# A routed expert kernel: the last 20 pairs of pages written twice, behind a branch on the page counts

## The chip, the cores and the metric

The kernel runs on one core of one Trainium2 chip. A core has TensorE (PE, matrix products), VectorE (DVE), ScalarE (ACT), GpSimd (POOL), SyncE (SP, here a queue of transfers) and 16 DMA engines. The metric is device time in microseconds (us), the median of the runs. One execution is taken by the hardware profiler; times inside it count from its first instruction.

## The reference

x has 8 batches of 512 tokens of width 256. A first layer (several normalizations with gathered tables and a small network) makes from each token a vector, and the second, of which the change speaks, sends it through 4 of 16 experts:

```python
probs = softmax(xf @ gate_w.T)
top_w, top_idx = top_k(probs, 4);  top_w /= sum(top_w)
h1, h3 = einsum('td,ehd->teh', xf, w1), einsum('td,ehd->teh', xf, w3)
eout = einsum('teh,edh->ted', silu(h1) * h3, w2)
x = x + sum over the 4 chosen of top_w * eout + a shared expert
```

All of it is in float32.

## The kernel before

The work has two stages. The first runs over the 8 batches, each of NJ = 4 tiles of 128 tokens; an order is planned by the class Plan, with costs and ranks, and written out for PE, DVE, ACT and SP. It ends with each tile's tokens routed. An expert's tokens stand in pages of 128 rows in a buffer xs_d in DRAM: a tile that fills an expert's page opens the next free one, so the pages of the experts lie mixed, in the order in which they were opened. The place of a token's k-th choice is in slot_all, and POOL scatters the normalized vectors there by indirect DMA. past_all keeps the number of pages opened so far. The experts can round up at most 16 x 127 rows, so after n tokens at most pages_after(n) = (4n + 16 x 127) // 128 pages are open: NPAGE = 143 at the end, and pages_for(b, j), which is 4t + 19 after tile t = 4b + j. Which expert owns a page is known only at run time, in page_e.

The second stage runs over pairs of pages, n_pair = 72 (the last has one page), in an order written out by hand in one loop. In pass i of the loop:

- experts(): before every other pair, PE, ACT and DVE load the experts' numbers of the next four pages into registers.
- load(): SP fetches four pages of xs_d (a quad), three quads ahead.
- turn(i + 2): PE transposes the pages (xt), ACT moves them out of PSUM with scale and bias (xtt).
- bring_weights(i + 2): ACT and DVE each copy one page's expert weights to a fixed place (wb).
- first(i): PE multiplies (hp), ACT makes silu, DVE multiplies the halves to g.
- second(i - 1): PE multiplies by w2 (yo), ACT copies yo to SBUF, and SP stores the two pages to ys_d.
- pick_weights(), in the first 32 passes: DVE gathers a tile's four routing weights.
- fetch(): POOL gathers 128 rows of ys_d for one tile and choice k by indirect DMA into a buffer yg. As its source is declared to be the first (pages_for - k) pages of ys_d, it waits for the stores of these and no others.
- weigh(): DVE adds weight times yg to x_all; after k = 0, SP writes the tile to the output.

There are 128 fetches in the order of tiles, k from 3 to 0. fetch_one() places the next one in the program if the pages that it needs are already stored at that place (stored[0]). It is called twice in each pass, before first() and before second(), and each fetch also waits for a mark there (xtt of pair i + 2, or g of pair i). There are eight buffers yg. weigh_due(i - 3) places the weigh() of the fetches that were placed three passes or more before. Each engine and each queue takes its instructions in order: on DVE a weigh() that waits for its fetch holds up the next wb and g, and on SP an output write that waits for weigh() holds up the next load and store. All indirect DMAs share POOL's queue, in order.

Line numbers of the rows below: L1515 xt, L1520 xtt, L1501 wb, L1539 hp, L1547 silu, L1559 yo, L1562 ACT's copy of yo, L1563 the store, L1447 the fetch, L1468 the output write; L192 is the helper through which all of DVE goes.

Of the kernel before, what the change touches and what calls it, by code (L numbers as in the profile page):

```python
# [9 lines left out]
F32 = mybir.dt.float32  # L10
BF16 = mybir.dt.bfloat16
I32 = mybir.dt.int32
AF = mybir.ActivationFunctionType
ALU = mybir.AluOpType
AX = mybir.AxisListType
# [4 lines left out]
P = 128  # L20
B, S, D = 8, 512, 256
E, HID, TOPK = 16, 128, 4
# [5 lines left out]
NJ = S // P  # L28
NC = D // P
# [23 lines left out]
def pages_for(b, j):  # L53

    return pages_after(b * S + (j + 1) * P)
# [11 lines left out]

NPAGE = pages_after(B * S)
QUAD = 4
NQUAD = -(-NPAGE // QUAD)  # L70


class Plan:
# [109 lines left out]
def adaln_ffn_kernel(ctx: ExitStack, tc: tile.TileContext, a: dict, out: bass.AP):  # L183
    nc = tc.nc
# [13 lines left out]
    vector = Recorded()  # L198
# [16 lines left out]
    pool_seq = {"single": None, "scatters": []}  # L215
# [24 lines left out]
    def start_after(name, i):  # L240

        tc.add_manual_dep(i.ins, marks[name], sync, reason="order of the transfers")
# [139 lines left out]
    if True:  # L382
# [49 lines left out]
        second = sp.tile([NROW, 4, D], BF16)  # L432
# [344 lines left out]
    with (  # L777
# [256 lines left out]

        flat = lambda v: v.rearrange("p a b -> p (a b)")
        by_tile = lambda v: v.rearrange("p e j -> p j e")
        turns = [0]

        def rank_d(b, g):

# [288 lines left out]
        for b in range(B):  # L1329
# [31 lines left out]
            t = b * T  # L1361
# [61 lines left out]
    def pick_weights(b, j):  # L1423
        eq = g2.tile([P, TOPK, E], F32, tag="eq", name=f"eq_{b}_{j}")
        vector.tensor_tensor(
            eq,
            pos_all[:, b, j].unsqueeze(1).to_broadcast([P, TOPK, E]),
            top_all[:, b, j, 0:TOPK].unsqueeze(2).to_broadcast([P, TOPK, E]),
            ALU.is_equal,
        )  # L1430
        vector.tensor_mul(
            eq, eq, ld[:, b * NJ + j].unsqueeze(1).to_broadcast([P, TOPK, E])
        )
        vector.reduce_sum(wk_all[:, b, j, :], eq, axis=AX.X)

    xs_v = xs_d.rearrange("(n p) d -> p n d", p=P)
    ys_v = ys_d.rearrange("(n p) d -> p n d", p=P)

    def pages_of_slot(b, j, k):

        return pages_for(b, j) - k

    def fetch(b, j, k, after):
        rows_ = pages_of_slot(b, j, k) * P
        yg = g2.tile([P, D], F32, tag="yg", name=f"yg_{b}_{j}_{k}", bufs=8)
        i = in_turn(
            nc.gpsimd.indirect_dma_start(  # L1447
                out=yg,
                out_offset=None,
                in_=ys_d[0:rows_, :],  # L1450
                in_offset=bass.IndirectOffsetOnAxis(ap=slot_all[:, b, j, k : k + 1], axis=0),
            )
        )
        if after:
            start_after(after, i)
        return yg

    def weigh(b, j, k, yg):
        vector.scalar_tensor_tensor(
            x_all[:, b, j, :],  # L1460
            yg,
            wk_all[:, b, j, k : k + 1],
            x_all[:, b, j, :],
            ALU.mult,
            ALU.add,
        )
        if k == 0:
            nc.sync.dma_start(out=out_v[b, :, j], in_=x_all[:, b, j])  # L1468
# [6 lines left out]

    def load(q):
        n = min(QUAD, NPAGE - q * QUAD)
        t = g2.tile([P, QUAD, D], F32, tag="xs", name=f"xs_{q}", bufs=4)
        nc.sync.dma_start(out=t[:, 0:n], in_=xs_v[:, q * QUAD : q * QUAD + n])
        loaded[q] = t  # L1480

    def experts(q):
        for engine in (PE, ACT, DVE):
            _, vs = nc.values_load_multi_w_load_instructions(
                page_e[0:1, q * QUAD : (q + 1) * QUAD],
                engines=[engine],
                min_val=0,
                max_val=(E - 1) * D,
                skip_runtime_bounds_check_because="an expert's number, or 0, times the width",
            )  # L1490
            values[q, engine] = vs
# [3 lines left out]
    def bring_weights(i):  # L1495
        for k, p in enumerate(pages_of(i)):
            v = values[p // QUAD, bring[k]][p % QUAD]
            brought[p] = g2.tile([P, NC, 2 * HID], F32, tag=f"wb{k}", name=f"wb_{p}", bufs=3)
            src = weights["w13"][:, :, bass.ds(v, 2 * HID)]
            if bring[k] == ACT:  # L1500
                nc.scalar.copy(brought[p], src)  # L1501
            else:
                vector.tensor_copy(brought[p], src)
# [4 lines left out]
    def turn(i):  # L1508

        src = loaded[2 * i // QUAD]  # L1510
        n = len(pages_of(i))
        pt = ps_t.tile([P, NC, 2, P], F32, tag=f"t{i % 2}", name=f"xt_{i}")
        for k, p in enumerate(pages_of(i)):
            for c in range(NC):
                nc.tensor.transpose(  # L1515
                    pt[:, c, k, :], src[:, p % QUAD, c * P : (c + 1) * P], ident
                )
        xt = g2.tile([P, NC, 2, P], F32, tag="xt", name=f"xtt_{i}", bufs=4)
        for c in range(NC):
            a_ = nc.scalar.activation(  # L1520
                xt[:, c, 0:n],
                pt[:, c, 0:n],
                AF.Identity,
                scale=vecs[:, V_INT_G, c : c + 1],
                bias=vecs[:, V_INT_BE, c : c + 1],
            )
        mark(("xt", i), a_)
        return xt
# [3 lines left out]
    def first(i, xt):  # L1532
        n = len(pages_of(i))
        pool, tag_ = ps_first[i % 4]
        ph = pool.tile([P, 2, 2, P], F32, tag=tag_, name=f"hp_{i}")
        for k, p in enumerate(pages_of(i)):
            for h in range(2):
                for c in range(NC):
                    nc.tensor.matmul(  # L1539
                        ph[:, h, k, :],  # L1540
                        brought[p][:, c, h * HID : (h + 1) * HID],
                        xt[:, c, k, :],
                        start=(c == 0),
                        stop=(c == NC - 1),
                    )
        g = g2.tile([P, 2, P], F32, tag="g", name=f"g_{i}", bufs=3)
        nc.scalar.activation(g[:, 0:n], ph[:, 0, 0:n, :], AF.Silu)  # L1547
        mark(("g", i), vector.tensor_mul(g[:, 0:n], g[:, 0:n], ph[:, 1, 0:n, :]))
        return g

    stored = [0]

    def second(i, g):
        n = len(pages_of(i))
        yo = g2.tile([P, 2, D], F32, tag="yo", name=f"yo_{i}", bufs=5)
        po = ps_o.tile([P, 2, D], F32, tag=f"o{i % 2}", name=f"yo_{i}")
        for k, p in enumerate(pages_of(i)):
            v = values[p // QUAD, PE][p % QUAD]
            nc.tensor.matmul(  # L1559
                po[:, k, :], g[:, k, :], w2[:, bass.ds(v, D)], start=True, stop=True  # L1560
            )
        nc.scalar.copy(yo[:, 0:n], po[:, 0:n])  # L1562
        nc.sync.dma_start(out=ys_v[:, 2 * i : 2 * i + n], in_=yo[:, 0:n])  # L1563
        stored[0] = 2 * i + n

    n_pair = -(-NPAGE // 2)
    for q in range(3):
        load(q)
    xt, g = {}, {}
    picks = [(b, j) for b in range(B) for j in range(NJ)]  # L1570
    fetches = [(b, j, k) for b in range(B) for j in range(NJ) for k in reversed(range(TOPK))]
    landed = []

    def fetch_one(i, after):

        if fetches:
            b, j, k = fetches[0]
            if stored[0] >= pages_of_slot(b, j, k) and (b, j) not in picks:
                landed.append((i, b, j, k, fetch(*fetches.pop(0), after)))
                return True  # L1580

    def weigh_due(by):

        while landed and landed[0][0] <= by:
            weigh(*landed.pop(0)[1:])

    experts(0)
    for t in range(2):
        bring_weights(t)
    for i in range(n_pair + 2):  # L1590
        if i % 2 == 0 and i // 2 + 1 < NQUAD:
            experts(i // 2 + 1)
        if i % 2 == 0 and i // 2 + 3 < NQUAD:
            load(i // 2 + 3)
        for t in range(3) if i == 0 else (i + 2,):
            if t < n_pair:
                xt[t] = turn(t)
        if i + 2 < n_pair:
            bring_weights(i + 2)

        if i + 2 < n_pair:
            fetch_one(i, ("xt", i + 2))
        if i < n_pair:
            g[i] = first(i, xt[i])
            fetch_one(i, ("g", i))
        if 0 <= i - 1 < n_pair:
            second(i - 1, g[i - 1])
        if picks:
            pick_weights(*picks.pop(0))
        weigh_due(i - 3 if i < n_pair else i)  # L1610
        while i >= n_pair and fetch_one(i, None):
            pass
    while landed or fetches:
        for _ in range(4):
            fetch_one(i, None)
        for _ in range(4):
            if len(landed) > 4 or landed and not fetches:
                weigh(*landed.pop(0)[1:])
# [58 lines left out]
```

## Time and profile before

| what | value |
|---|---|
| median of 3 runs | 506.04 us (505.32 to 507.46) |
| the profiled execution | 506.59 us |
| its span, first to last instruction | 504.9 us |
| mean granted clock of TensorE | 0.978 of full |
| PE busy | 476.4 us, 94% |
| DVE, ACT, POOL busy | 359.8, 291.4, 295.8 us |
| first and last fetch | 300.21 and 496.84 us |
| last weigh() begins | 499.73 us |

The span is a little shorter than the execution's own time, which holds what lies around it. The profile is read by stage: busy shares over the whole span mix a first stage with the pair loop (from about 267.5 us) and a tail behind PE's last product. A row of a timeline has the start, the length, the engine (PEld is the loading of weights, SPq a DMA issue on SP), line, operation, and in brackets how long the engine was idle before and what ended that.

### The profile page before, as it was taken

The page shows a single profiled execution, that of the slowest core. Times are in us where ns is not written, and L with a number is a line of the kernel's source. Part 1 is how long each engine was busy: PE and PEld are TensorE (multiplying, and loading weights), DVE is VectorE, ACT ScalarE, POOL GpSimd, SP SyncE. Part 2 cuts the span into 40 slices and gives each one's busy share as a digit, 9 for nine tenths or more (in the row PEclk, how much of TensorE's full clock was granted, in tenths as well). Part 3 has the DMA queues.
Part 4 walks back from the last instruction along what each step waited for, and adds up shares of the span by engine and source line. Part 5 has one row for each costly group of instructions (what it writes and reads, how often), then busy time and mean ns, then how long its engine had stood idle before and what let it go on. Part 6 is the DMA issues. An engine that isn't in the chain of part 4 may idle for free.

```text
span 504.9 us, 9488 instructions
## 1 busy us (share of the span) xinstructions
PE 476.4 (94%) x2764; PEld 358.8 (71%) x2764; DVE 359.8 (71%) x1459; ACT 291.4 (58%) x584; POOL 295.8 (59%) x320
## 2 busy tenths in 40 slices
PE   5989899999999999999998999999999999999970
PEld 2547556465656655456658999999999999999970
DVE  7997899999979788867846445777755455555552
ACT  5741643636654615133137777777777777777750
POOL 8615504777677777777750006556666576665673
PEclk8999899999999999999999999999999999999995
DMA  7749959879974758372235557889899899899773
GB/s 222 276 142 323 362 178 296 269 242 273 322 248 143 209 180 235 134 270 105 95 107 167 173 175 247 253 284 288 249 292 282 265 287 289 263 284 282 228 219 108
DMA packets 108153, 116.99 MB, mean 232 GB/s; under 512 B 9029, under 2 KB 95807, under 8 KB 108103
## 3 DMA queue, kind: packets, MB, share of 16 engines
q1 hardware_dynamic: 92942, 74.39, 47.5%
q0 software_dynamic: 14848, 41.96, 26.4%
q8 instruction: 22, 0.36, 0.3%
q14 instruction: 28, 0.23, 0.2%
q10 hardware_dynamic: 313, 0.05, 0.1%
HBM read 57.91 MB, written 58.46 MB: 230 GB/s over the span
## 4 chain that ended last, share of the span: by engine, by line
PE 67%; DVE 21%; DMA 7%; issue 2%; ACT 1%; POOL 1%; POOLq 0%; SPq 0%; DVEq 0%; ACTq 0%
PE hp L1539 25%; PE yo L1559 12%; PE ph L920 10%; PE xt L1515 6%; PE sh L753 5%; DVE pw L192 3%; DVE cat L192 3%; PE pz L940 3%; PE so L769 3%; DMA pw<-in_pw_dram,idx 2%; DMA x_all<-in_x_dram 1%; DVE st_x L192 1%; DVE st_h L192 1%; DMA xs_d<-z,slot_all 1%; DVE z L192 1%
## 5 line engine op out<-in xcount | busy, mean ns | idle before, releaser
L1447 POOL DMA_INDIRECT yg<-ys_d,slot_all x128 | 125.9, 983 | 111.0 <-ACT yo L1562 49.9
L1125 POOL DMA_INDIRECT xs_d<-z,slot_all x128 | 125.6, 982 | 41.9 <-issue 13.9
L1539 PE MATMUL hp<-xtt,wb 128*128 128x128 f32 x1144 | 139.5, 275 | 0.0
L1539 PEld LDWEIGHTS hp<-xtt,wb 128*128 128x128 f32 x1144 | 133.6, 192 | 0.1
L192 DVE TENSOR_TENSOR g<-g,hp 128x256 f32<-128x256 f32 x72 | 30.2, 419 | 82.9 <-ACT g L1547 82.8
L920 PE MATMUL ph<-cat,iws 128*128 128x512 f32 x192 | 88.9, 593 | 0.0
L1520 ACT ACTIVATE xtt<-xt,vecs 128x256 f32<-128x256 f32 x144 | 73.5, 566 | 3.2 <-PE xt L1515 3.2
L1559 PE MATMUL yo<-w,g 128*128 x286 | 73.7, 380 | 0.0
L192 DVE SCALAR_TENSOR_TENSOR x_all<-yg,wk_all,x_all 128x256 f32<-128x256 f32 x128 | 59.5, 482 | 10.7 <-DMA yg<-ys_d,slot_all 9.5
L920 PEld LDWEIGHTS ph<-cat,iws 128*128 128x128 f32 x192 | 35.9, 190 | 38.0 <-issue 33.2
L1562 ACT COPY yo<-yo 128x512 f32<-128x512 f32 x72 | 41.9, 583 | 33.9 <-PE yo L1559 26.2
L793 POOL DMA_INDIRECT pw<-in_pw_dram,idx x32 | 31.7, 992 | 44.6 <-ACT cat L903 32.1
L1559 PEld LDWEIGHTS yo<-w,g 128*128 128x128 f32 x286 | 48.8, 191 | 3.9 <-DVE g L192 0.2
L1501 ACT COPY wb<-w 128x512 f32 x72 | 44.6, 621 | 0.0
L1515 PE MATMUL xt<-ident,xs 128*128 128x128 f32 x286 | 42.9, 273 | 0.7 <-ACT xtt L1520 0.7
L1515 PEld LDWEIGHTS xt<-ident,xs 128*128 128x128 f32 x286 | 35.6, 141 | 7.9 <-ACT xtt L1520 0.9
L1547 ACT ACTIVATE g<-hp 128x256 f32<-128x256 f32 x72 | 27.6, 383 | 15.3 <-PE hp L1539 15.1
L940 PE MATMUL pz<-iw,hid 128*128 128x272 f32 x128 | 34.2, 404 | 0.0
L192 DVE COPY wb<-w 128x512 f32 x71 | 31.3, 443 | 3.4 <-issue 2.2
L820 ACT ACTIVATE z<-z,nb_z,rs_z 128x256 f32<-128x256 f32 x32 | 16.7, 588 | 27.7 <-DVE nb_z L192 27.7
L920 PE MATMUL ph<-catx,iws 128*128 128x512 f32 x64 | 30.3, 595 | 0.0
L820 ACT ACTIVATE pw<-pw,nb_h,rs_h 128x256 f32<-128x256 f32 x32 | 16.9, 590 | 21.4 <-DVE nb_h L192 21.3
(217 smaller groups left out, 668.9 us busy)
## 6 DMA issues: line engine op xcount, KB each, us to landing
ys_d<-yo SPq DMA_DIRECT2D x71, 256.0 KB, 2.2
xs<-xs_d SPq DMA_DIRECT2D x35, 512.0 KB, 5.6
xs_d<-zero SPq DMA_DIRECT2D x8, 2048.0 KB, 11.1
x_all<-in_x_dram SPq DMA_DIRECT2D x8, 512.0 KB, 3.9
w<-in_w_dram SPq DMA_DIRECT2D x32, 128.0 KB, 4.6
out_dram<-x_all SPq DMA_DIRECT2D x32, 128.0 KB
xs_d<-z,slot_all POOLq DMA_INDIRECT x128, 2.9
w<-in_w_dram SPq DMA_DIRECT2D x4, 512.0 KB, 8.8
```

Of the source, the lines that this page charges most:

```text
L192: i = getattr(nc.vector, op)(*args, **kwargs)
L820: nc.scalar.activation(dst, src, AF.Identity, scale=rs[:, j : j + 1], bias=nb[:, j : j + 1])
L920: nc.tensor.matmul(res[b]["ph", m], l, r, start=(q == 0 and i == 0), stop=(q == 3 and i == len(mm) - 1))
L940: nc.tensor.matmul(pz, hid[:, m, js], iw2[:, m, :], start=(m == 0), stop=(m == NC - 1))
L1125: i = nc.gpsimd.indirect_dma_start(out=xs_d[0 : pages_for(b, j) * P, :], out_offset=bass.IndirectOffsetOnAxis(ap=slot_all[:, b, j, k : k + ...
L1447: nc.gpsimd.indirect_dma_start(out=yg, out_offset=None, in_=ys_d[0:rows_, :], in_offset=bass.IndirectOffsetOnAxis(ap=slot_all[:, b, j, k : ...
L1501: nc.scalar.copy(brought[p], src)
L1515: nc.tensor.transpose(pt[:, c, k, :], src[:, p % QUAD, c * P : (c + 1) * P], ident)
L1520: a_ = nc.scalar.activation(xt[:, c, 0:n], pt[:, c, 0:n], AF.Identity, scale=vecs[:, V_INT_G, c : c + 1], bias=vecs[:, V_INT_BE, c : c + 1],)
L1539: nc.tensor.matmul(ph[:, h, k, :], brought[p][:, c, h * HID : (h + 1) * HID], xt[:, c, k, :], start=(c == 0), stop=(c == NC - 1),)
L1559: nc.tensor.matmul(po[:, k, :], g[:, k, :], w2[:, bass.ds(v, D)], start=True, stop=True)
L1562: nc.scalar.copy(yo[:, 0:n], po[:, 0:n])
```

## The change

The second stage is cut at pair FORK = 48. Pairs 0 to 47 stay as one program; what follows is written twice, as the two ways of a branch.

count_over() takes, in pass 2, for each of the tiles 20 to 31 (from batch B_FORK = 5 on) the number of pages opened up to there less a limit usual_for(t): 4t + 13, at most 132, and 136 for the last tile. The largest of the differences, plus 143, goes to over_i; all five engines load it into a register at the fork and compare.

- If no count is over its limit, run_rest(USUAL // 2) runs pairs 48 to 67, and pages 136 to 142, which are then empty, are not worked on. The fetches of tiles 20 to 31 use the limit usual_for(t) - k in place of pages_for - k.
- Otherwise run_rest(n_pair) runs pairs 48 to 71 with the old limits.

The bookkeeping of the placing (state, turns, the order on POOL) is copied at the fork, so that both ways start from the same. Since both must use the same buffers, tiles drawn from pools become slices of fixed ones: yg (12 places in place of 8), xs, wb, xt, g; yo has 4 buffers in place of 5.

The loop of the second stage has moved into run_pairs(). fetch_one() is now called three times at the end of a pass, after second() and weigh_due(), and no longer waits for a mark; it places nothing while 12 fetches are not yet weighed. At the end, what is left of fetches and weigh() follows in run_rest().

```diff
+USUAL = 136
+FORK = 48
+B_FORK = 5
+def usual_for(t):
+    return USUAL if t == B * NJ - 1 else min(4 * t + 13, USUAL - 4)
+N_YG = 12
...
+    yg_all = g2.tile([P, N_YG, D], F32, bufs=1)
+    xs_all = g2.tile([P, 4, QUAD, D], F32, bufs=1)
+    wb_all = g2.tile([P, 3, 2, NC, 2 * HID], F32, bufs=1)
+    xt_all = g2.tile([P, 4, NC, 2, P], F32, bufs=1)
+    g_all = g2.tile([P, 3, 2, P], F32, bufs=1)
...
-    def fetch(b, j, k, after):
-        rows_ = pages_of_slot(b, j, k) * P
-        yg = g2.tile([P, D], F32, tag="yg", name=f"yg_{b}_{j}_{k}", bufs=8)
+    def fetch(b, j, k, n_pages):
+        rows_ = n_pages * P
+        yg = yg_all[:, turns[0] % N_YG]
+        turns[0] += 1
...
-        if after:
-            start_after(after, i)
...
-        yo = g2.tile([P, 2, D], F32, tag="yo", name=f"yo_{i}", bufs=5)
+        yo = g2.tile([P, 2, D], F32, tag="yo", name=f"yo_{i}", bufs=4)
...
+    in_turn(
+        nc.gpsimd.iota(
+            over_i, pattern=[[4, n_last]], base=usual_for(B_FORK * NJ), channel_multiplier=0
+        )
+    )
+    def count_over():
+        vector.tensor_single_scalar(over, over_i, float(USUAL - 4), ALU.min)
+        vector.memset(over[:, n_last - 1 :], float(USUAL))
+        pages = past_all[0:1, B_FORK % 4 :, :, E - 1].rearrange("p b j -> p (b j)")
+        vector.tensor_sub(over, pages, over)
+        vector.reduce_max(over[:, 0:1], over, axis=AX.X)
+        vector.tensor_single_scalar(over_i[:, 0:1], over[:, 0:1], float(NPAGE), ALU.add)
...
+    def fetch_one(i):
+        fetches = state["fetches"]
+        if not fetches or len(state["landed"]) == N_YG:
+            return False
+        if state["stored"] >= fetches[0][0] and fetches[0][1:3] not in picks:
+            n, *which = fetches.pop(0)
+            state["landed"].append((i, *which, fetch(*which, n)))
+            return True
...
+    def run_pairs(i0, i1, end):
+        for i in range(i0, i1):
...
+            if i < end:
+                g[i] = first(i, xt[i])
+            if 0 <= i - 1 < end:
+                second(i - 1, g[i - 1])
+            if picks:
+                pick_weights(*picks.pop(0))
+            if i == 2:
+                count_over()
+            weigh_due(i - 3)
+            for _ in range(3):
+                fetch_one(i)
+    def run_rest(end):
+        run_pairs(FORK, end + 1, end)
+        landed = state["landed"]
+        while state["fetches"]:
+            if len(landed) == N_YG:
+                weigh(*landed.pop(0)[1:])
+            fetch_one(end)
+        weigh_due(end)
...
-        if i + 2 < n_pair:
-            fetch_one(i, ("xt", i + 2))
-        if i < n_pair:
-            g[i] = first(i, xt[i])
-            fetch_one(i, ("g", i))
...
+    run_pairs(0, FORK, n_pair)
+    is_over = nc.values_load(over_i[:, 0:1], min_val=0, max_val=2 * NPAGE, ...)
+    with tc.If(is_over < NPAGE + 1) as usual:
+        state["fetches"] = sorted(
+            (min(n, usual_for(b * NJ + j) - k) if b >= B_FORK else n, b, j, -k)
+            for n, b, j, k in state["fetches"]
+        )
...
+        run_rest(USUAL // 2)
...
+    with usual.Else():
+        run_rest(n_pair)
```

## The prediction

> **What bounds the kernel now.** I read the forty slices of the page first: TensorE is at nine or ten tenths from the fourth slice to the thirty-eighth. The change touches only the second half (the loop over pairs of pages), so I took the table of stretches next.
>
> ```profile
> core 0: us, PE busy (x) PEld busy (x) DVE busy (x) ACT busy (x) POOL busy (x), PEclk, DMA share, GB/s
> ...
> 416.00:447.00 31.00, 31.00 (x242) 29.48 (x242) 16.76 (x40) 24.06 (x50) 19.54 (x20) 1.00 0.89 276
> ...
> 490.00:505.00 15.00, 0.00 (x0) 0.00 (x0) 4.17 (x9) 0.04 (x1) 5.96 (x7) 0.59 0.42 128
> ```
>
> In the pair loop PE is busy for the whole stretch at full granted clock (1.00); DVE and ACT have room, the 16 DMA engines are 0.89 busy. In the last 15 us PE does nothing: a tail with a bound of its own. The timeline of PE gives the length of a pair (xt, hp, yo in each):
>
> ```profile
> 472.39 0.60 PE L1515 MATMUL xt<-ident,xs 128*128 128x128 f32 x4
> ...
> 475.48 0.60 PE L1515 MATMUL xt<-ident,xs 128*128 128x128 f32 x4
> 475.92 1.95 PE L1539 MATMUL hp<-xtt,wb 128*128 128x128 f32 x16
> 477.70 1.03 PE L1559 MATMUL yo<-w,g 128*128 x4
> 478.57 0.60 PE L1515 MATMUL xt<-ident,xs 128*128 128x128 f32 x4
> ```
>
> 478.57 - 475.48 = 3.09 us a pair, 1.545 a page. Pair 66, from 472.39, is an even one and starts with the register loads of the experts' numbers; it takes 3.09 too, so these are hidden. The last yo ends at 489.6. The tail, in the timeline of POOL, DVE and SP:
>
> ```profile
> 489.01 1.07 POOL L1447 DMA_INDIRECT yg<-ys_d,slot_all  x1 [0.45 <-DVE g L192]
> 490.38 0.95 POOL L1447 DMA_INDIRECT yg<-ys_d,slot_all  x1 [0.30 <-DVE x_all L192]
> ...
> 496.84 0.95 POOL L1447 DMA_INDIRECT yg<-ys_d,slot_all  x1 [0.30 <-issue]
> ...
> 499.73 0.48 DVE L192 SCALAR_TENSOR_TENSOR x_all<-yg,wk_all,x_all 128x256 f32<-128x256 f32 x1 [0.70 <-DMA yg<-ys_d,slot_all]
> 500.24 0.33 SPq L1468 DMA_DIRECT2D out_dram<-x_all  x1
> ```
>
> POOL issues fetches back to back: 16 steps from 475.79 to 496.84 are 21.05 us, 1.32 each, and 7 from 463.90 to 472.97 are 1.30 each (0.95 busy, 0.30 between, some longer); I take 1.30. So the tail is set by POOL's backlog, not by PE: the last fetch goes out 7.2 us after PE's end, and 8.06 us later the span ends (504.9). These two engines, PE up to 489.6 and POOL behind it, must both be followed. One more line, of the writers and readers of yg between 416 and 470 us, is needed below:
>
> ```profile
> DMA to landing us min/median/max: 3.3/4.5/6.0
> ```
>
> **Does the branch take the short way?** Routing the reference's inputs by its own formula, tile by tile, I count 135 pages in use of 143, and after each of tiles 20 to 31 at most the limit that the change compares with (margins 0 to 2 pages). So the short way with 68 pairs is taken.
>
> **1. Seven pages left out.** Before, pages 136 to 142 cost PE 7 x 1.545 = 10.8 us. PE's last yo moves from 489.6 to 478.8. The stores and loads of these pages go too; they were hidden.
>
> **2. The fetches.** Number them f = 0 to 127. Before, fetch f needs f + 16 pages stored, and a place in the program comes one pair late (it counts the stores of the pair before the last, and waits for marks on xt or g); 8 buffers. After, up to the fork at pair 48, the limit is the same but the place comes one pair earlier; there are 12 buffers. From the fork f needs f + 10 (tiles 20 to 29) or f + 9 (30 and 31). Counting through both loops: at the fork 79 are out and 49 left; pairs 48 to 53 issue three each, 54 to 64 two each, 65 three, 66, 67 and 68 two each.
> POOL's clock: pair 48 starts at 478.57 - 20 x 3.09 = 416.8 (call it S). In any pair, second() of the pair before ends 3.25 after the start (478.73 - 475.48), ACT's copy 0.65 later, and the store lands 2.3 later when the DMA is quiet (a step of the chain that ended last) or 3.3 (the median of these stores from 478 on); under load I take 3.3: 7.2 after the start. Pair 47's two fetches then leave POOL free at S - 3.09 + 7.2 + 2.6 = S + 6.7; with 0.5 for the branch, 7.2. Fetch m of the 49 can go at S + 7.2 + 1.30 m. m = 40, the first of pair 65, would go at S + 59.2; its store lands at S + 17 x 3.09 + 7.2 = S + 59.7. So by then POOL has just caught up, and the eight after it follow at 1.30: 416.8 + 59.7 + 8 x 1.30 = 486.9 for the last. Before it was 496.84: 9.9 less. The last store lands at 478.8 + 0.65 + 2.3 = 481.8 and so does not decide.
>
> **3. What the burst does to DVE.** weigh() waits in order on DVE, in front of wb and of the next g, for which PE's second() waits; SP's out writes wait for weigh(), and the next store stands behind them in SP's queue. In an ordinary pair (two fetches): the second lands at 7.2 + 1.3 + 4.5 = 13.0; its weigh() stands at 3 x 3.09 + 3.26 + 0.48 = 13.0. No wait worth naming, and if DVE is late, PE suffers only when g of the next pair, 0.48 + 0.42 + 0.42 behind, misses 5 x 3.09 + 2.2 = 17.7: 3.4 us of cover. In the burst POOL loses 3 x 1.30 - 3.09 = 0.8 us a pair. Worst is the third fetch of pair 53, m = 17: out at S + 29.3, landed at 33.8, weigh, wb and g done at 35.1; PE wants it at S + 10 x 3.09 + 2.2 = 33.1. PE stalls 2.0 us in all. From the landing times' ends, 3.3 gives 0.8 and 6.0 gives 3.5. A stall moves every later store, so the 59.7 of step 2 becomes 61.7: the gain is 9.9 - 2.0 = 7.9.
>
> **4. The branch.** Per engine one register load, waiting on semaphores of pair 2's count (long fulfilled), and a compare. Row first: the even pair above has such a load on PE, ACT and DVE and is not longer, so beside PE's queued yo (0.9 us) it costs 0; on POOL I put 0.5. The Trainium skill speaks against this: "Runtime: NRT & Kernel Launch", section Instruction fetch mechanics, says that a taken branch whose target is outside the two-page window stalls for a DMA fetch of instructions, and calls runtime control flow expensive. Such a fetch would have the price of a DMA, 2.3 to 3.3 us by the stores above, into engines that are 0.89 busy. By that rule the sum would be a gain of 5 to 6, as PE's cover is gone after 0.9; by the row 7.9. I take the row, as the short way stands directly behind the compare in the program on every engine; no run here shows a branch, so 3 us stays in the range. The jump over the other way at the end lies beside the last out write on SP.
>
> **5. At nothing.** One iota on POOL (0.2, after the scatters, when it idles 39 us for the first store) and some six small DVE operations in pair 2 (about 0.2 each like the eq rows; DVE idles 1.5 us a pair there). yo with 4 buffers instead of 5: a buffer is wanted again after 12.4 us, its store lands in 3.3. Fixed slices instead of pools keep the counts; up to the fork the order on PE and ACT is what it was, and up to pair 2 on the others. Six bare semaphore steps on SP even out the shorter way: below 0.1 each, SP waits most of each pair for ACT.
>
> **Sum.** Against the profiled execution, 506.59 with a span of 504.9: 504.9 - 7.9 = 497.0, and with the 1.7 around it 498.7. It lies 0.55 above the median of the runs, 506.04, so the median of the new kernel is 498.1; I say **498.0 us**.
>
> **Rivals.**
> - *The burst is swallowed.* Landings nearer 3.3, or steps of 1.25: no stall, and the last fetch goes at 486.9 or, with POOL free, two steps after the last store, 483 to 484. Gain 10 to 13: 493 to 496. For it: in the whole stretch from 300 to 490 DVE waited only 3.5 us for fetches. Against: 0.89 of the DMA is taken, and three fetches a pair add more.
> - *Branch and burst both cost.* Instruction fetch by step 4 and landings of 6 us: gain 7.9 - 1.5 - 3 = 3.4, so 502 to 503.
> - *The change doesn't do what it says.* A near tie routed otherwise on the chip opens a page more at a tile with margin 0, and the long way runs: 72 pairs, 506 +- 2.
> - *Slower: the loop from store to fetch to weigh to g becomes the bound of every pair.* The place in the program is one pair earlier now, with no pause between fetches; all 60 pairs from 8 on are in it. It has 3.4 us of cover; past that each us costs 1/5 us a pair, 12 us over 60 pairs. It eats the 7.9 when landing and store together take 3.4 + 0.7 = 4.1 us more than the medians. The longest landing seen is 1.5 above the median, which speaks against; that the pacing by marks is gone speaks for. At 4.5 us more, 1.1 x 12 - 7.9 makes it 5.3 slower: 511.
>
> **How the numbers follow.** Forecast (gain 5.5 to 10): 0.58. Burst swallowed: 0.20. Branch and burst cost (gain 2.5 to 5.5): 0.09. Long way or a gain lost otherwise: 0.06. Slower: 0.07. About 0.5%, 2.5 us, is what a measurement of this kernel can tell from none: faster 0.87, within 0.06, slower 0.07. The range of 8 in 10 reaches from 494.0 (most of the swallowed case) to 502.5 (branch and burst).
>
> **What would show it.** Right: PE's last yo 8 to 10 us earlier; 49 fetches behind the fork with pauses only from pair 60 on; a wait of DVE on fetches grown from 3.5 to some 10 us, and PE gaps of 2 us in pairs 52 to 58 only; last fetch some 8 us after PE's end. Wrong: a PE gap of over 1 us right at pair 48 (branch), pairs longer than 3.09 before the fork (loop), a last hp of pair 71 (long way), or POOL waiting for stores throughout (burst swallowed).

## The result, and the profile after

| kernel | median us (runs) | profiled execution, span | ratio to before, 95% interval |
|---|---|---|---|
| before, beside it | 506.61 (505.32 to 507.55) | 506.59, 504.9 | |
| after | 508.26 (505.86 to 510.77) | 509.45, 507.6 | 1.0037 (1.0022 to 1.0053) |

The forecast was 498.0. The change makes the kernel slightly slower, although PE has seven pages less to do. The same two stretches, from the table of stretches of the kernel after:

```profile
core 0: us, PE busy (x) PEld busy (x) DVE busy (x) ACT busy (x) POOL busy (x), PEclk, DMA share, GB/s
...
416.00:447.00 31.00, 30.11 (x231) 28.13 (x231) 17.53 (x43) 22.91 (x48) 22.04 (x23) 1.00 0.92 286
...
490.00:508.00 18.00, 0.66 (x4) 0.23 (x2) 4.85 (x10) 0.71 (x2) 7.41 (x8) 0.64 0.43 124
```

Before, PE was busy for all of 31.00 us at clock 1.00. Now 0.89 is missing at the same clock: PE has idle time inside the loop. The timeline of PE of the kernel after shows where:

```profile
350.33 0.60 PE L1532 MATMUL xt<-ident,xs_all 128*128 128x128 f32 x4
...
353.42 0.60 PE L1532 MATMUL xt<-ident,xs_all 128*128 128x128 f32 x4
356.24 1.13 PE L1574 MATMUL yo<-w,g_all 128*128 x4 [0.44 <-DVE g_all L207]
357.21 0.60 PE L1532 MATMUL xt<-ident,xs_all 128*128 128x128 f32 x4
```

The pair from 350.33 takes 3.09 us, the next 3.79, and PE's yo waited for g from DVE. Read so from pair to pair, ten pairs ahead of the fork take 3.1 to 4.3 us (5.1 us lost in all), the one at the fork 4.41 (1.3 lost), and four behind it 3.5 to 4.72 (4.1 lost). In the kernel before, every pair of this stretch takes 3.09. With the seven pages (-10.8), a first stage that ended 1.05 later in this execution and a tail 1.7 longer, that is -10.8 + 5.1 + 1.3 + 4.1 + 1.05 + 1.7 = +2.5; the spans differ by 2.7.

What DVE, POOL and PE waited for between 300 and 490 us (total, number of times, longest), first in the kernel before, then after:

```profile
DVE g L192 <- ACT g L1547: 68.2, 60, 1.7
...
DVE x_all L192 <- DMA yg<-ys_d,slot_all: 3.5, 4, 1.7
...
POOL yg L1447 <- DMA ys_d<-yo: 0.9, 3, 0.3
```

```profile
DVE x_all L207 <- DMA yg_all<-ys_d,slot_all: 59.9, 46, 2.9
...
POOL yg_all L1466 <- DMA ys_d<-yo: 27.5, 19, 3.6
...
PEld yo L1574 <- DVE g_all L207: 8.2, 14, 1.6
PE yo L1574 <- DVE g_all L207: 5.1, 10, 1.4
```

Before, DVE's slack was spent on waiting for ACT, which costs nothing. After, it is spent on fetches, 46 times instead of 4, and some of it reaches PE. The chain is stores, fetch, weigh(), g, yo. One turn of it in the timelines of SP, POOL and DVE after (stores, fetches and weigh() are matched by counting each from 0 at the loop's first; fetches 27 and 28, at 347.35 and 348.60, need store 21, at 341.41, and the weigh() at 354.90 is number 28):

```profile
340.73 0.39 SPq L1496 DMA_DIRECT2D xs_all<-xs_d  x1
341.41 0.36 SPq L1578 DMA_DIRECT2D ys_d<-yo  x1
...
347.35 0.94 POOL L1466 DMA_INDIRECT yg_all<-ys_d,slot_all  x1 [1.51 <-DMA ys_d<-yo]
348.60 0.94 POOL L1466 DMA_INDIRECT yg_all<-ys_d,slot_all  x1 [0.30 <-issue]
...
354.90 0.48 DVE L207 SCALAR_TENSOR_TENSOR x_all<-yg_all,wk_all,x_all 128x256 f32<-128x256 f32 x1 [2.42 <-DMA yg_all<-ys_d,slot_all]
355.77 0.41 DVE L207 TENSOR_TENSOR g_all<-g_all,hp 128x256 f32<-128x256 f32 x1
```

Store to first fetch takes 5.94 us, the second fetch goes out 1.25 later, from there to weigh() it takes 6.30, and g ends at 356.18, just ahead of the late yo at 356.24: 14.77 us from the store. The prediction's terms for this turn are 3.3, 1.3, 4.5 and 1.3, together 10.4, and its cover ends 13.75 us behind the store (17.65 - 3.9, as the store goes out 3.25 + 0.65 after the pair's start). So here the store took 2.6 more and the fetch 1.8 more, which is more than the cover.

By the same count over all stores from pair 8 to pair 47, a pair's first fetch goes out 3.0 to 3.5 us behind its store in pairs 8 to 12, where the fetches begin; the median is 5.4 for even pairs and 6.0 for odd ones, and around pairs 37 to 39 it reaches 8.9. It is the time to the fetch's issue, so it takes in POOL being busy; in the kernel before it is 4.7 and 5.0, though hardly any fetch waits for its store there. In 15 of these first fetches after, POOL did wait for the store itself: 13 of them belong to odd pairs, and from pair 14 on they go out 5.3 to 6.4 us behind it.

What sets the odd ones apart stands in SP's queue. First before, then after:

```profile
386.70 0.36 SPq L1563 DMA_DIRECT2D ys_d<-yo  x1
387.16 0.42 SPq L1479 DMA_DIRECT2D xs<-xs_d  x1
389.79 0.36 SPq L1563 DMA_DIRECT2D ys_d<-yo  x1
390.25 0.42 SPq L1468 DMA_DIRECT2D out_dram<-x_all  x1
```

```profile
359.74 0.35 SPq L1485 DMA_DIRECT2D out_dram<-x_all  x1
360.18 0.39 SPq L1496 DMA_DIRECT2D xs_all<-xs_d  x1
361.11 0.36 SPq L1578 DMA_DIRECT2D ys_d<-yo  x1
```

Before, store, load, store, output write follow each other, and a store comes 2.6 us behind the load of 512 KB. Since the fetches stand one place earlier, the weigh() with k = 0 now falls into the odd passes. The output write then stands ahead of the next pass's load, and the load ahead of the store: when weigh() is late, the output write is late, the load goes out 0.4 us behind it and the store 0.9 us behind the load. That closes a circle: a late weigh() makes the next store late. In pairs 9 and 11 the load still stands 2.6 us ahead of the store and POOL's fetch goes out 3.3 and 3.5 us behind it; in the odd waits from pair 17 on the load stands 0.5 to 2.1 us ahead and it is 5.6 to 6.4. (The DMA share grows too, from 0.75 between 300 and 330 us to 0.87 between 330 and 360.) What the order is worth is measured below.

The tail, from the timelines of PE, POOL and DVE after, and the landing times of yg's writers and readers between 416 and 470 us:

```profile
488.43 2.22 PE L1574 MATMUL yo<-w,g_all 128*128 x8
```

```profile
495.40 0.94 POOL L1466 DMA_INDIRECT yg_all<-ys_d,slot_all  x1 [0.92 <-DMA ys_d<-yo]
...
499.20 0.94 POOL L1466 DMA_INDIRECT yg_all<-ys_d,slot_all  x1 [0.30 <-issue]
```

```profile
502.12 0.48 DVE L207 SCALAR_TENSOR_TENSOR x_all<-yg_all,wk_all,x_all 128x256 f32<-128x256 f32 x1 [0.43 <-DMA yg_all<-ys_d,slot_all]
```

```profile
DMA to landing us min/median/max: 3.5/4.8/7.0
```

PE's last yo ends at 490.65 (489.62 before), the last fetch goes out 8.55 us later. The landing median is 4.8 instead of 4.5, and between 300 and 410 us 4.9 instead of 4.4.

### The profile page after: what moved, and what is told of

Its sections match the earlier page's. It is cut to its first block, busy times and chain, and to the rows that moved or that the text cites. A ratio compares the mean times of both kernels' runs of the same rounds, so it can differ in the third digit from the quotient of the medians.

```text
span 507.6 us, 9215 instructions
## 1 busy us (share of the span) xinstructions
PE 471.8 (93%) x2678; PEld 349.3 (69%) x2680; DVE 356.7 (70%) x1457; ACT 282.4 (56%) x564; POOL 295.0 (58%) x321
## 3 DMA queue, kind: packets, MB, share of 16 engines
q1 hardware_dynamic: 91054, 72.56, 46.8%
## 4 chain that ended last, share of the span: by engine, by line
PE 46%; DVE 22%; DMA 18%; issue 6%; ACT 3%; POOL 3%; POOLq 1%; DVEq 0%; ACTq 0%
PE hp L1556 12%; PE ph L935 9%; DMA yg_all<-ys_d,slot_all 9%; PE yo L1574 6%; PE sh L768 5%; DMA ys_d<-yo 5%; DMA pw<-in_pw_dram,idx 4%; PE xt L1532 3%; DVE pw L207 3%; DVE cat L207 3%; PE so L784 3%; POOL yg_all L1466 3%; PE pz L955 2%; DVE st_x L207 1%; DVE st_h L207 1%
## 5 line engine op out<-in xcount | busy, mean ns | idle before, releaser
L1466 POOL DMA_INDIRECT yg_all<-ys_d,slot_all x128 | 125.1, 977 | 113.0 <-PE xt L1532 39.1
L1556 PE MATMUL hp<-xt_all,wb_all 128*128 128x128 f32 x1088 | 132.6, 275 | 0.0
L1556 PEld LDWEIGHTS hp<-xt_all,wb_all 128*128 128x128 f32 x1088 | 127.0, 192 | 0.1
L207 DVE SCALAR_TENSOR_TENSOR x_all<-yg_all,wk_all,x_all 128x256 f32<-128x256 f32 x128 | 60.7, 483 | 68.6 <-DMA yg_all<-ys_d,slot_all 67.6
L1574 PE MATMUL yo<-w,g_all 128*128 x272 | 71.5, 386 | 5.3 <-DVE g_all L207 5.1
L1537 ACT ACTIVATE xt_all<-xt,vecs 128x256 f32<-128x256 f32 x136 | 69.4, 566 | 5.9 <-PE xt L1532 4.5
L1574 PEld LDWEIGHTS yo<-w,g_all 128*128 128x128 f32 x272 | 46.4, 191 | 11.7 <-DVE g_all L207 8.2
L1532 PE MATMUL xt<-ident,xs_all 128*128 128x128 f32 x272 | 40.8, 273 | 2.0 <-ACT yo L1577 0.8
L1518 ACT COPY wb_all<-w 128x512 f32 x68 | 42.1, 621 | 0.0
L1532 PEld LDWEIGHTS xt<-ident,xs_all 128*128 128x128 f32 x272 | 33.5, 141 | 9.6 <-issue 1.9
## 6 DMA issues: line engine op xcount, KB each, us to landing
xs_d<-zero SPq DMA_DIRECT2D x8, 2048.0 KB, 10.4
```

The source lines that it names most:

```text
L207: i = getattr(nc.vector, op)(*args, **kwargs)
L1466: nc.gpsimd.indirect_dma_start(out=yg, out_offset=None, in_=ys_d[0:rows_, :], in_offset=bass.IndirectOffsetOnAxis(ap=slot_all[:, b, j, k : ...
L1532: nc.tensor.transpose(pt[:, c, k, :], src[:, p % QUAD, c * P : (c + 1) * P], ident)
L1537: a_ = nc.scalar.activation(xt[:, c, 0:n], pt[:, c, 0:n], AF.Identity, scale=vecs[:, V_INT_G, c : c + 1], bias=vecs[:, V_INT_BE, c : c + 1],)
L1556: nc.tensor.matmul(ph[:, h, k, :], brought[p][:, c, h * HID : (h + 1) * HID], xt[:, c, k, :], start=(c == 0), stop=(c == NC - 1),)
L1574: nc.tensor.matmul(po[:, k, :], g[:, k, :], w2[:, bass.ds(v, D)], start=True, stop=True)
```

## The experiments

The theory after the traces: the distance from a store to the weigh() behind it has become one pair (3.09 us) too short, and SP's order makes it worse. Rivals: the branch; the marks that no longer pace the fetches; the three fetches a pair behind the fork. Runs with the label e1 to e4 were made beside a kernel before of 506.94 us, those from e5b to e8b beside 506.93, and e9 and e10 beside 507.03.

**Without the branch.** The short way stands straight behind pair 47; the long way is left out.

```diff
-    is_over = nc.values_load(over_i[:, 0:1], ...)
-    with tc.If(is_over < NPAGE + 1) as usual:
...
-        run_rest(USUAL // 2)
+    run_rest(USUAL // 2)
-    with usual.Else():
-        run_rest(n_pair)
```

> The changed kernel without the branch: the short way (68 pairs, tighter limits) follows pair 47 directly, and no engine loads or compares a count. The kernel would be wrong for inputs that open more pages. Branch theory (each engine loses instruction fetches at the fork): back to 500 or less, if the branch is what ate the gain. Queue theory (the quad's load stands directly ahead of the store in SP's queue, the store lands late, the fetch and weigh behind it too) and cover theory (fetches placed one pair earlier leave weigh too little time): only the 1.3 us that pair 48 is longer than 3.09 comes back, 506.5 to 507.5.

Measured: 508.22 us, ratio 1.0014 (1.0000 to 1.0028), against 508.26 and 1.0037 (1.0022 to 1.0053) for the whole change. The medians agree; the two ratios leave the branch between nothing and some 2 us. The loss is still there without it: the pair at 48 takes 3.09, but the next 4.35, and PE's pairs lose 10.1 us in all against 10.5. In the runs below that keep the branch and have the distance, the pair at the fork takes 3.09 like all others.

**The load behind the store.** In the kernel after, load() stands behind second() in its pass.

```diff
-            if i % 2 == 0 and 2 * (i // 2 + 3) < end:
-                load(i // 2 + 3)
...
             if 0 <= i - 1 < end:
                 second(i - 1, g[i - 1])
+            if i % 2 == 0 and 2 * (i // 2 + 3) < end:
+                load(i // 2 + 3)
```

> The changed kernel with one step moved: in even passes the load of a quad is written behind second(), so on SP the store goes ahead of the load; nothing else moves. Queue theory: pairs before the fork go back to 3.09, a good part of the 4 us behind it too, DVE's waits on fetches fall from 60 us to some 20; 498 to 502. Cover theory: the store lands a little earlier but the place is still one pair early, so no more than 2 us come back: 506 to 508.

Measured: 504.86 us, ratio 0.9961 (0.9944 to 0.9978); 3.4 less than after. DVE still waits 56.8 us for fetches in 54 places, but all pairs ahead of the fork except one take 3.09. The profiled execution, of 501.99 us, is the quickest of 20 (to 508.34), so its pairs may flatter the kernel. The order alone is less than half of what is missing.

**One pair later.** In the kernel after, the three calls of fetch_one() stand ahead of second() and so count one store less.

```diff
+            for _ in range(3):
+                fetch_one(i)
             if 0 <= i - 1 < end:
                 second(i - 1, g[i - 1])
...
             weigh_due(i - 3)
-            for _ in range(3):
-                fetch_one(i)
```

> The changed kernel with its three fetches of a pass placed ahead of second(), not behind it: each fetch then counts only the stores up to the pair before, as the kernel before did, and the output writes fall into the other pass, away from the load. It undoes place and order together. Queue theory and cover theory both: pairs before the fork at 3.09, 498 to 501, and if the two add, faster than the kernel with the load moved. If the loss were in the branch or in the burst of three fetches alone: 506 or more.

Measured: 499.53 us, ratio 0.9846 (0.9829 to 0.9863), 7.4 below before. Every pair ahead of the fork takes 3.09; behind it PE loses 1.3 us. Fetches still have no marks and still come in threes behind the fork, so with the full distance these two rivals explain at most that 1.3. SP's queue reads store, load, store, output write again, so distance and order came back together.

**Early place on the kernel before.** Two fetches at the end of each pass without marks, 12 buffers yg and 4 yo; nothing else.

```diff
-        if i + 2 < n_pair:
-            fetch_one(i, ("xt", i + 2))
...
-            fetch_one(i, ("g", i))
...
         weigh_due(i - 3 if i < n_pair else i)
+        for _ in range(2 if i < n_pair else 0):
+            fetch_one(i, None)
```

> The kernel before with the early place alone: two fetches at the end of each pass, behind second() and weigh, no marks; 12 buffers for yg and 4 for yo, as in the changed kernel. No branch, no page left out, no tighter limits. Queue and cover theory: the loss of pairs 8 to 47 in the changed kernel (5 us) appears here and goes on to pair 71: 511 to 516. Branch or burst theory: 505 to 507.

Measured: 512.84 us, ratio 1.0116 (1.0089 to 1.0143). Without branch, left-out pages or tighter limits, the early place costs 5.9 us.

**weigh() one pass later.** e5b, e6b, e7b and e8b ran a second time under these labels. Their first runs were on another chip, where the kernel before took 582.75 us (577.2 to 592.44), and they took 582.54, 582.82, 586.66 and 582.07, with intervals of 0.7 to 1% to either side; only the third stood clear of 1, at 1.0089 (1.0016 to 1.0161), and did not hold below. The early place stays:

```diff
-            weigh_due(i - 3)
+            weigh_due(i - 4)
```

> The changed kernel with weigh() four passes behind its fetch instead of three; place and order of the fetches on GpSimd stay early. It makes DVE wait for a fetch one pair (3.09 us) later, and puts SP's out writes behind the store of an even pass instead of ahead of the load. Theory (distance from store to weigh, and the order on SP): 499 to 501 us, pairs of 3.09 before the fork, DVE's wait for fetches below 25 us. Rival (the missing pacing by marks, which stays missing): 505 to 508 us. On a chip on which the kernel before took 582.75 us this one took 582.54, which decided nothing.

Measured: 499.68 us, ratio 0.9842 (0.981 to 0.9874), as with the late place. The same view of waits as above, of this kernel:

```profile
DVE x_all L207 <- DMA yg_all<-ys_d,slot_all: 20.5, 24, 3.0
...
PEld yo L1574 <- DVE g_all L207: 1.5, 4, 0.6
```

POOL issues as early as in the kernel after, and the pairs ahead of the fork are all 3.09 again. So it is not the early issue that hurts, but the early weigh(). The first fetch goes out 4.5 (even) and 4.8 us (odd) behind its store instead of 5.4 and 6.0. SP's queue again reads store, load, store, output write, with 2.6 us from load to store, so this run too gives back distance and order together; the next ones part them. What it keeps can't be the main cause either: 4 buffers yo, 12 yg, and the fixed slices.

**The order alone, on the kernel before.** The load goes into the odd passes; SP's queue reads store, output write, load, store, as after.

```diff
-        if i % 2 == 0 and i // 2 + 3 < NQUAD:
+        if i % 2 == 1 and i // 2 + 3 < NQUAD:
             load(i // 2 + 3)
```

> The kernel before with the load of a quad of pages in the odd passes instead of the even ones (one pair later, three pairs ahead of its first use): SP's queue then reads store, out, load, store as in the changed kernel, while the fetches keep their place, marks and distance. Theory, order alone costs: 508 to 511 us, DVE's wait for fetches above 20 us. Rival, order only costs where the fetch stands a pair too early: 506 to 507 us. On the chip with 582.75 us for the kernel before it took 586.66 (ratio 1.0089, 1.0016 to 1.0161), which leans to the first.

Measured: 506.86 us, ratio 0.9999 (0.999 to 1.0007). The waits of this kernel hardly differ from those of before:

```profile
DVE x_all L192 <- DMA yg<-ys_d,slot_all: 4.7, 8, 1.1
```

The theory that the order alone costs fell here: with the full distance it costs nothing.

**The distance alone, on the kernel before.** weigh_due(i - 2) in place of weigh_due(i - 3); in the second run with the load in the odd passes too, which restores SP's order of before.

```diff
-        weigh_due(i - 3 if i < n_pair else i)
+        weigh_due(i - 2 if i < n_pair else i)
```

> The kernel before with one number changed: weigh() two passes behind its fetch instead of three. Place, marks, limits and pages stay as before; the distance from store to weigh is one pair (3.09 us) shorter, as in the changed kernel, and the out writes fall into the odd passes, so that SP's queue reads out, load, store. If the shorter distance is the cause: 510 to 514 us, pairs longer than 3.09 in the whole loop, DVE's wait for fetches above 50 us. If the missing pacing by marks or the burst is: 506 to 507.5 us.

> The same shorter distance, with the loads of quads in the odd passes too, so that SP's queue has the order of the kernel before again (store, load, store, out). With distance 3 the other order alone gave 506.86 us, no change; so this is the fourth corner. If the order makes up about half of the loss where the distance is short: 508 to 510 us, two or more below the run with the short distance alone. If the distance is all: within 1 us of it. If the distance costs nothing in the right order: 506 to 507 us.

Measured: 513.54 us, ratio 1.0133 (1.0109 to 1.0157), and with the order restored 508.58, ratio 1.0027 (1.0012 to 1.0042); the profiled execution of the second is one of its quicker ones, 507.18 of 506.85 to 509.59. Waits of the first, then of the second:

```profile
DVE x_all L192 <- DMA yg<-ys_d,slot_all: 60.7, 51, 2.8
...
PEld yo L1559 <- DVE g L192: 3.8, 4, 1.4
PE yo L1559 <- DVE g L192: 3.0, 4, 1.2
```

```profile
DVE x_all L192 <- DMA yg<-ys_d,slot_all: 46.8, 54, 2.1
...
PEld yo L1559 <- DVE g L192: 0.2, 1, 0.2
```

With that the kernel before has been run at both distances in both orders:

| us against before | store, load, store, output | output, load, store |
|---|---|---|
| weigh() 3 passes behind | 0 | -0.1 |
| weigh() 2 passes behind | +1.6 | +6.5 |

Together they cost more than the sum of each alone: the short distance costs 1.6 in the old order, where PE hardly waits for g (0.2 us), and 6.5 where the output write and the load stand ahead of the store. The 6.5 needs no branch, no tighter limits, no lost marks and no left-out page, and lies near the 5.9 of the early place.

**Without the tighter limits.** The late place, and behind the fork each fetch waits for its old limit or for page 136.

```diff
-            (min(n, usual_for(b * NJ + j) - k) if b >= B_FORK else n, b, j, -k)
+            (min(n, USUAL) if b >= B_FORK else n, b, j, -k)
```

> The late place without the tighter limits behind the fork: each fetch waits for its old limit, or for page 136 where that is less; the pages are still left out. Theory (POOL's backlog sets the tail): no burst, so 1.3 us of longer pairs go; nine fetches are left for the time after the last store near 483.5, the last goes out at 493.6 instead of 491.2: 502 us (501 to 504). Rival (the burst costs as much as it brings): 499 to 500 us.

Measured: 505.86 us, ratio 0.9984 (0.9976 to 0.9992), 3.9 more than I expected. All pairs take 3.09, and PE's last yo ends 211.5 us after the first xt, where before it was 222.1: the seven pages are gone from PE, 10.6 us. But the span falls by nothing like it. From POOL's timeline:

```profile
484.57 0.94 POOL L1466 DMA_INDIRECT yg_all<-ys_d,slot_all  x1 [1.59 <-DMA ys_d<-yo]
...
497.32 0.95 POOL L1466 DMA_INDIRECT yg_all<-ys_d,slot_all  x1 [0.30 <-issue]
```

Eleven fetches, not the nine I had counted, are left after the last wait for a store, and ten steps of 1.275 end at 497.32. Of the 7.4 us of the late place, the pages alone bring 1.1 and the tighter limits on top of them 6.3: they let POOL do these fetches while PE still works. (Limits without the left-out pages were not run.)

**A faster version.** The late place, the fork at pair 40, tighter limits from tile 16 on, and at most seven fetches in three passes behind the fork.

```diff
-FORK = 48
+FORK = 40
-B_FORK = 5
+B_FORK = 4
-    return USUAL if t == B * NJ - 1 else min(4 * t + 13, USUAL - 4)
+    return USUAL if t == B * NJ - 1 else min(4 * t + (13 if t >= 20 else 15), USUAL - 4)
...
+        vector.tensor_single_scalar(over[:, 0:4], over[:, 0:4], 2.0, ALU.add)
...
+            for _ in range(2 + (i % 3 == 0) if i >= FORK else 3):
+                fetch_one(i)
```

> A version meant to be faster: the late place, the fork at pair 40 instead of 48, tighter limits from tile 16 on (4t + 15 for tiles 16 to 19), and behind the fork at most seven fetches in three passes, so that GpSimd (1.27 us each) is not asked for more than 2.43 a pair. Theory (POOL's backlog from pair 48 on sets the last fetch, 491.2 with the late place, and its burst costs PE 1.3): POOL catches up near pair 60, the last two fetches follow the last store near 484: 494 to 496.5 us. Rival (the tail hangs on the out writes and the DMA, not on POOL): 498 to 499.5 us.

Measured: 497.24 us, ratio 0.9811 (0.9791 to 0.9832), faster than both kernels, 0.7 above what I expected. From POOL's timeline:

```profile
464.38 1.15 POOL L1466 DMA_INDIRECT yg_all<-ys_d,slot_all  x1 [0.77 <-DVE g_all L207]
...
487.39 1.08 POOL L1466 DMA_INDIRECT yg_all<-ys_d,slot_all  x1 [0.30 <-issue]
```

No pair is longer than 3.09 and POOL does catch up, with pauses near pairs 61 to 63. From 464.38 on it has none, so the last fetch still goes out behind a backlog, at 487.39 and not near 485.

## Why the prediction was wrong

- **The branch** takes the short way (68 pairs) and costs PE nothing that shows in the pair at the fork, which takes 3.09 in the late place and with the later weigh(); the row was right. By the rule that the prediction weighed against it (the Trainium skill, "Runtime: NRT & Kernel Launch", Instruction fetch mechanics: a taken branch out of the window stalls for a fetch of instructions) its estimate of 2.3 to 3.3 us would have to show there, and in the times (508.22 without it, 508.26 with it). Whether the short way counts as a taken branch, no run here shows. The signs named for its cost, a gap of over 1 us right at pair 48, did appear (4.41 us), but the cause was another: the gap is absent where the distance is restored and the branch kept.
- **Step 1** holds: 10.6 us measured in place of 10.8, in the run without the tighter limits, where no pair is late.
- **Step 2** has the mis-sized term. "The store lands 2.3 later when the DMA is quiet ... or 3.3 ...; under load I take 3.3". The 3.3 was one landing, in the tail, where no loads run. In the loop of the kernel before hardly any fetch waits for a store (0.9 us in all), so its profile showed no landing where it mattered. It did hold an upper bound, which I did not read: 4.7 and 5.0 us from a store to its first fetch at the median, 1.4 and 1.7 above the 3.3. After, it measured 5.4 and 6.0.
- **Step 3** is the one that failed: "No wait worth naming". In its own working, 7.2 becomes 9.3 to 9.9, and the second fetch lands at 15.1 to 15.7 while its weigh() stands at 13.0. That takes 2.1 to 2.7 of the 3.4 us of cover in an ordinary pass, in place of none, and leaves about 1 us for all variation; in the turn shown above there was none left. DVE waited for fetches 59.9 us in 46 places, where some 10 us were forecast. I followed weigh() on DVE and wrote down that the next store stands behind the output write on SP, but did not ask what the earlier place does to the order of the loads there, though it moves each output write by one pass. With that order the short distance costs 6.5 us and not 1.6.
- **The burst** itself was sized fairly: 2.0 us predicted, 1.3 and 1.5 measured with the distance restored (late place, later weigh()). On top of the short distance it is 4.1.
- **The sum without the failed step** holds: a gain of 7.9 predicted, 7.4 and 7.3 measured in the two runs that give back one pair of distance and with it SP's order. The whole loss is 508.26 - 499.6 = 8.7. In the profiled execution PE's pairs show it as 5.1 ahead of the fork, 1.3 at it, and 4.1 - 1.4 = 2.7 behind it beyond the burst, 9.1 in all. The 5.9 and 6.5 of the kernel before are for its whole loop and are not a part of this sum.
- **The rival on the slower side** named this mechanism, and its sign, pairs longer than 3.09 ahead of the fork, came; but it was put as needing 4.1 us of lateness from store and landing together. The turn shown above has 4.4 (2.6 and 1.8). I argued against it with the longest landing of a fetch alone, 1.5 above the median, where the store's time grew by more, and left out SP's order, by which one late weigh() makes the next store late. At a chance of 0.07 it was held too unlikely.

What is not separated: how much of the loss at the fork and behind it in the kernel after is the burst on POOL and how much the store behind the load, since no run had the short distance, the new order and a smaller burst together. Nor is the time from store to fetch split into landing and POOL's own backlog, save in the 15 waits named above.

## What to carry to other kernels

When an edit moves the place of one step in a hand-ordered loop, list what it does to the distance of every consumer and to the order in every queue that the consumer feeds, and size each transfer in the stage where it will run: a wait that nobody makes in the profile of before leaves its duration unknown, not small. Moving a producer earlier without moving its consumer later gains nothing if the consumer is placed by counting from the producer. If a measured gain is missing, give the distance back by one step at the consumer and look again.

## What I had not expected of the hardware

- The order of load and store on one queue costs 5 us (513.54 against 508.58) with the short distance and nothing (506.86 against 506.93) with the full one.
- With the short distance DVE waits 46.8 us for fetches (in an execution of 507.18) and the kernel is only 1.6 us slower at the median: a wait on an engine with slack is not a loss until it reaches the bound engine.
- On the chip of 582.75 us the kernel with the later weigh() showed DVE idle in 15 places before g with no releaser that the profile names, up to 6.7 us at a time; its waits for the whole execution have the line below, and in the same kernel at 499.68 us there is no such line. In one of these places, g at 376.71, ACT's silu had ended just before, at 376.67, and ACT had itself waited 2.19 us for PE's hp: the other engines were late too. The runs don't show why.

```profile
DVE g_all L207 <- issue: 49.7, 15, 6.7
```
